# Two graph attention layers on one core: a transpose put ahead of the scores, the norm done in pairs, x split in five pieces, and a limit on list parts

## The chip, the core and the metric

The kernel runs on one core of a Trainium2 chip. A core has TensorE (PE in the profile; PEld is its loading of weights), VectorE (DVE), ScalarE (ACT), GpSimd (POOL) and SyncE (SP), which here issues the transfers. The engines run side by side, each through its own list of instructions in order, and wait for one another through semaphores. The metric is the device time of one execution in microseconds (us); lower is better.

## The reference

Sixteen graphs (batches) of 1024 nodes, 64 features each, with an adjacency matrix `adj` in which a node has itself and a handful of neighbours. Two layers, each with a residual and a layer norm without weights:

```python
# layer 0: attention with 8 heads of 64, over the neighbours only
q, k, v = (x @ Wq + bq), (x @ Wk + bk), (x @ Wv + bv)        # per head
scores  = leaky_relu(q k^T / 8 + edge_bias[edges], 0.2)       # -1e9 where edges == 0
out     = softmax(scores) v
x       = layernorm(x + out @ Wp + bp)
# layer 1: additive attention, one head
hp = x @ lin_w^T + lin_b;  u = hp @ W1^T;  w = hp @ W2^T
e  = sum_f a_f * leaky_relu(u_i + w_j, 0.2)                   # -9e15 where adj == 0
x  = layernorm(x + elu(softmax(e) hp))
```

## The kernel before

The kernel never forms 1024 x 1024 scores. For every batch it reads the adjacency matrix once and makes a list of neighbours for each node. Then both layers gather the listed neighbours with matmuls against indicator matrices and work on 120 slots for each group of nodes.

**Lists.** `prepare(b)` makes the lists of batch b in 41 pieces: it reads `adj` (L324, L327), folds it with matmuls (`pat`, L333, L338), finds the largest keys by pairs of MAX8 and MATCH_REPLACE (L344/L345, later L377/L379), turns keys into columns (L352 to L367, tiles `left`, `flags`) and writes out columns and slots. `finish(b)` makes the `mask` (L427 to L442).

**Gathering.** A layer needs x in three bf16 parts, whose sum is x in full precision: `thirds` (L451 cast, L453 what is left, five GpSimd instructions). For every tile t of 128 nodes `indicate` makes the indicator tiles `f` on VectorE (L475, two of [128 x 2176]), `gather` runs the matmuls with the parts (L499) in two halves, `own` copies each node's own column (L484, GpSimd), and `turn` transposes what was gathered (L518).

**Layer 0, tile t.** `queries` (L586, L587), `score` (matmuls L603, then on VectorE `sc` L611, `ls` L619, `mx` L620), `exps` (ACT, L629), `divide` (reciprocal L636 on VectorE, product L637 on GpSimd, in two halves 0 and 1), `turn_weights` (L645, L647), `attend` (L655), for every second tile `heads` (`po`, L671), `rows` (L687), and `residual` (L693, then `look`: BN statistics L544, L545). `end()` runs `Norm.scale` on the whole batch: four GpSimd instructions L549 (add), L550 (pow), L551 (subtract), L552 (multiply), and gives `x1`.

**Layer 1, tile t.** `own_rows` (`ub`, L728, GpSimd), `project` (`pz` L740 and L746, then `r` on ACT L751 and VectorE L752), `weigh` (`e`, L766, then its maximum `m1`, L768), `exps` (L774), `turn_weights` (transpose `pt1` L780, copy `eT` on VectorE L782), `attend` (`pa`, L791), `rows` and `residual` (L804, L805). `end()` is a generator: ELU, residual (L819, L820), `look` for all tiles, `Norm.scale`, output.

**Order.** The order on every engine is written out by hand in one loop over g = 0 to 146, under a manual schedule. Batch and tile are `b, t = divmod(g, 8)`. Layer 0 works on tile g and finishes it up to three steps later; layer 1 runs LAG = 12 steps behind (u = g - 12). At five places in each step, `lists.place(g, k)` puts in pieces of the next lists, up to a due number (3 to 6 a step by `QUOTA`, two steps ahead), and one piece of the first generator in `lists.side` (`finish`, or layer 1's `end`). `Layer0(b + 1)` is created at the end of t = 6 and `Layer1(b - 1)` at the end of t = 2; the constructor calls `begin`, which transposes x (`px`, L274) and makes the three parts.

Three PSUM tiles share one single bank, tag "e" of the pool `ps_z`: `back` (the rows of both layers), `e` in `weigh`, and `pt1` in `turn_weights`. A tile gets it when the readers of the tile before are through. The middle of a step, as written before the change:

```python
lists.place(g, 1)
at(l1, u, "gather", 0)
at(l0, g - 1, "turn")
lists.place(g, 2)
at(l1, u - 1, "weigh")
...
at(l1, u, "gather", 1)
...
at(l0, g - 2, "turn_weights")
at(l1, u - 2, "turn_weights")
at(l1, u - 1, "turn")
```

Of the kernel before, what the change touches and what calls it, by code (L numbers as in the profile page):

```python
# [24 lines left out]
WIN = 34  # L25
# [8 lines left out]
def kernel(  # L34
# [244 lines left out]
            for n in range(2):  # L279
                nc.tensor.matmul(ps[sub(n), t, :], src[:, ts(t, D)], w(n), start=True, stop=True)  # L280

    started, edges, masks, late = {}, {}, {}, {}

    def start(b):

        xs = dbl.tile([P, NT, D], F32, tag="xs", bufs=3, name=f"xs_{b}")
        dg = sml.tile([P, NT], I32, tag="dg", bufs=2, name=f"dg_{b}")
        diag = adj[b].rearrange("r c -> (r c)")[0 : N * N : N + 1]
        for n in range(2):
            nc.sync.dma_start(xs[sub(n), :, :], by_rows(x[b], n))  # L290
# [15 lines left out]
        started[b] = xs, dg, ads, load  # L306

    def prepare(b):

        if b not in started:  # L310
            start(b)
        xs, dg, ads, load = started.pop(b)
# [99 lines left out]
        for n in range(2):  # L412
            for q in range(NQ):
# [6 lines left out]
        edges[b] = (xs, col_d)  # L420
        late[b] = (flags, dg, rows_s)

    def finish(b):

        flags, dg, rows_s = late.pop(b)
        mask = dbl.tile([P, NT, SLOTS], BF16, tag="mask", bufs=4, name=f"mask_{b}")
# [8 lines left out]
        nc.vector.tensor_scalar(mask[:, :, 2 * CAP2 : SLOTS], own, 0.0, NEG, ALU.is_equal, ALU.mult)  # L435
        yield
        nc.vector.tensor_scalar(dgf, dg, 2.0, None, ALU.is_ge)
        nc.vector.tensor_reduce(flags[:, 18:19], dgf, XX, ALU.max)
        fl = sml.tile([P, 1], F32, tag="fl", bufs=2, name=f"fl_{b}")
        nc.vector.tensor_reduce(fl, flags, XX, ALU.max)  # L440
        nc.vector.tensor_scalar(fl, fl, 0.5, None, ALU.is_ge)
        nc.vector.tensor_tensor(bad, bad, fl, ALU.max)  # L442
        masks[b] = mask

    def thirds(src, tag, nm):

        t3 = dbl.tile([P, 3, NT, D], BF16, tag=tag, bufs=3, name=f"{tag}_{nm}")
        rest = src
        less = per.tile([P, NT, D], F32, tag="less", name=f"less_{tag}_{nm}")
        for k in range(3):  # L450
            nc.gpsimd.tensor_copy(t3[:, k, :, :], rest)  # L451
            if k < 2:
                nc.gpsimd.tensor_tensor(less, rest, t3[:, k, :, :], ALU.subtract)  # L453
                rest = less
        return t3

    class Tiles:


        def load(self, t):  # L460
            nm = f"{self.b}_{self.layer}_{t}"
            self.cb[t] = cb = dbl.tile([P, NSEG, 2, NQ, WIN], BF16, tag="cb", bufs=3, name=f"cb_{nm}")
            nc.sync.dma_start(
                cb.rearrange("p s n q k -> p (s n q k)"),
                self.col_d[t].rearrange("s n q k -> (s n q k)").unsqueeze(0).to_broadcast([P, NSEG * 2 * NQ * WIN]),
            )

        def indicate(self, t):
# [52 lines left out]
        def begin(self, x_):  # L521

            b = self.b
            px = ps_g.tile([P, 512], F32, tag="g", name=f"px{self.layer}_{b}")
            columns_T(px, x_)
            self.xT = dbl.tile([P, 512], F32, tag=f"xT{self.layer}", name=f"xT{self.layer}_{b}")
            nc.scalar.copy(self.xT, px)
            self.t3 = thirds(x_, "x3", f"{self.layer}_{b}")
            self.f, self.xg, self.xn = {}, {}, {}

    def banks(tag, name):

# [2 lines left out]
    class Norm:  # L535
# [8 lines left out]
            nc.vector.bn_stats(s6, y[:, t, :])  # L544
            nc.vector.bn_aggr(self.mv[:, t, :], s6)  # L545

        def scale(self, dst, y):
            rs = sml.tile([P, NT], F32, tag="rs", name=f"rs_{self.nm}")
            nc.gpsimd.tensor_tensor(rs, self.mv[:, :, 1], eps.to_broadcast([P, NT]), ALU.add)  # L549
            nc.gpsimd.tensor_tensor(rs, rs, root.to_broadcast([P, NT]), ALU.pow)  # L550
            nc.gpsimd.tensor_tensor(dst, y, self.mv[:, :, 0:1].to_broadcast([P, NT, D]), ALU.subtract)  # L551
            nc.gpsimd.tensor_tensor(dst, dst, rs.unsqueeze(2).to_broadcast([P, NT, D]), ALU.mult)  # L552

    class Layer0(Tiles):
        layer = 0

        def __init__(self, b):
            self.b, self.cb, (self.xs, self.col_d) = b, {}, edges[b]
            self.begin(self.xs)
            self.mx = dbl.tile([P, 2, NG // 4], F32, tag="mx", name=f"mx_{b}")  # L560
            self.y = dbl.tile([P, NT, D], F32, tag="y", name=f"y0_{b}")
            self.norm = Norm(f"0_{b}")
            self.qp, self.ls, self.den, self.w = {}, {}, {}, {}

# [125 lines left out]
        def residual(self, t):  # L690
            if t % 2 == 0:
                return
            nc.vector.tensor_tensor(self.y[:, t - 1 : t + 1, :], self.pr, self.xs[:, t - 1 : t + 1, :], ALU.add)  # L693
            for t_ in (t - 1, t):
                self.norm.look(self.y, t_)

        def end(self):
            x1 = dbl.tile([P, NT, D], F32, tag="x1", name=f"x1_{self.b}")
            self.norm.scale(x1, self.y)

            low = sml.tile([P, 1], F32, tag="low", bufs=2, name=f"low_{self.b}")
            nc.vector.tensor_reduce(low, self.mx.rearrange("p n g -> p (n g)"), XX, ALU.max)
            nc.vector.tensor_scalar(low, low, -NEG / 100.0, None, ALU.is_gt)
            nc.vector.tensor_tensor(bad, bad, low, ALU.max)
            return x1

    class Layer1(Tiles):
        layer = 1

        def __init__(self, b, x1):  # L710
            self.b, self.cb, self.x1, (_, self.col_d) = b, {}, x1, edges[b]
# [5 lines left out]
        def sums(self):  # L717
            pu = ps_g.tile([P, NT, D], F32, tag="g", name=f"pu_{self.b}")
            for t in range(NT):
                for n in range(2):  # L720
                    nc.tensor.matmul(pu[sub(n), t, :], self.xT[:, ts(t, D)], w1h[:, n, :], start=True, stop=True)
            self.u = dbl.tile([P, NT, D], F32, tag="u", name=f"u_{self.b}")
# [86 lines left out]
        def end(self):  # L809
# [10 lines left out]
            nc.gpsimd.tensor_tensor(y, y, self.x1, ALU.add)  # L820
            yield
            norm = Norm(f"1_{b}")
            for t in range(0, NT, 2):
                norm.look(y, t)
                norm.look(y, t + 1)
                yield
            norm.scale(o, y)
            yield
            for n in range(2):
                nc.sync.dma_start(by_rows(out[b], n), o[sub(n), :, :])  # L830

# [14 lines left out]
    class Lists:  # L846
# [11 lines left out]
        def place(self, g, k):  # L858
            b, t = divmod(g + AHEAD, NT)
            due = PIECES * b + sum(QUOTA[:t]) + QUOTA[t] * (k + 1) // PLACES  # L860
            last = k == PLACES - 1
            while self.done < due and self.part != ("keys" if last else "sums"):
                self.part = next(self.work, None)
                self.done += 1
            while self.side:
# [6 lines left out]
    with tc.manual_schedule(engines={getattr(mybir.EngineType, e) for e in order}):  # L872
        for _ in prepare(0):
            pass
        for _ in finish(0):
            pass
        l0[0] = Layer0(0)
        l0[0].constants()
        l0[0].load(0)
        l0[0].load(1)  # L880
# [2 lines left out]
        for g in range(NT * B + LAG + 7):  # L883
            u = g - LAG
            b, t = divmod(g, NT)
            if t == 0 and 0 < b < B:
                lists.side.append(finish(b))
            lists.place(g, 0)
            at(l0, g - 2, "exps", 0, range(4))
            at(l0, g - 1, "score", lambda: at(l0, g - 2, "divide", 0))  # L890
            if (g - 1) // NT not in l0:
                at(l0, g - 2, "divide", 0)
            at(l0, g - 2, "exps", 1, range(2))
# [4 lines left out]
            back = ps_z.tile([P, 3, D], F32, tag="e", name=f"back_{g}") if g > 3 else None  # L898
            at(l1, u - 3, "rows", back)
            at(l0, g - 3, "rows", back)  # L900
            at(l0, g, "queries")
            at(l1, u - 3, "residual")
            at(l0, g - 3, "residual")
            if t == 6 and b - 2 in l1:
                lists.side.append(l1[b - 2].end())
            at(l0, g - 2, "divide", 1)
            at(l1, u - 1, "project")
            lists.place(g, 1)
            at(l1, u, "gather", 0)
# [7 lines left out]
            if t == 2 and b - 1 in l0:  # L917
                x1 = l0[b - 1].end()
            at(l0, g - 2, "turn_weights")
            at(l1, u - 2, "turn_weights")  # L920
            at(l1, u - 1, "turn")
            lists.place(g, 3)
            at(l1, u + 1, "indicate")
# [433 lines left out]
```

## Time and profile before

| | |
|---|---|
| median of 3 runs | 2505.18 us (2500.58 to 2507.12) |
| the profiled execution | 2508.74 us, its span 2506.8 us |
| granted TensorE clock in it | 0.988 of full speed |
| busy time of PE, DVE, ACT, POOL | 92%, 80%, 58%, 36% of the span |
| costliest VectorE line | f, L475: 512 instructions, 491.6 us |
| costliest GpSimd line | ls, L637: 256 instructions, 285.8 us |
| longest waits of PE in the loop | po for sc 27.7 us, e for r 17.7 us, pz for sc 17.1 us |

The profile is one execution. A line of a timeline gives the start, the duration, the engine, the line of the kernel, the operation, `out<-in` by tile names with shapes, and in brackets the idle time before it with what ended it. A line of windows gives for one stretch its length and the busy time of each engine with the number of instructions, then the granted clock and the share of the DMA engines. A table of waits names who waited for whom, the total, the count and the longest.

### The profile page before, as it was taken

Reading aid. Unit: us, or ns where it says so; the run is one execution under the profiler, and the core shown is the slowest. Engines: PE = TensorE matmul, PEld = TensorE weight load, DVE = VectorE, ACT = ScalarE, POOL = GpSimd, SP = SyncE. Lnnn points to the kernel's source line nnn. Section 1 sums busy time; section 2 is a strip of 40 time slices with the busy share of each in tenths; the row PEclk is TensorE's granted clock in tenths of the full one; section 3 lists DMA queues with packets and bytes.
Section 4 is the critical chain, followed back from the end, with each engine's and each line's share of the span. In section 5 each row is a group of like instructions: output and inputs, shape, how many; then the busy total and the mean of one; then the engine's idle time right before and its main releaser. Section 6 shows DMA issues by size and latency. Waiting matters only on the chain. (4 is left out here: it accounts for less than half of the span.)

```text
span 2506.8 us, 110853 instructions
## 1 busy us (share of the span) xinstructions
PE 2308.1 (92%) x48706; PEld 1957.7 (78%) x48706; DVE 2012.1 (80%) x5237; ACT 1445.2 (58%) x4401; POOL 912.9 (36%) x1106
## 2 busy tenths in 40 slices
PE   5387999999999999999999999999999999999986
PEld 3376788878788887878788787888878888888864
DVE  6687879888888988888898888889888888876642
ACT  0154656656565665656566566656656665666743
POOL 1133333434334343433434343342434434243331
PEclk9998999999999999999999999999999999999998
DMA  3412332423233242323324232332423233221210
GB/s 102 122 59 89 104 103 78 133 77 116 73 102 108 78 133 80 114 73 107 103 78 133 84 109 75 106 103 78 133 86 108 81 100 106 62 92 57 66 52 18
DMA packets 190543, 230.66 MB, mean 92 GB/s; under 512 B 91492, under 2 KB 157092, under 8 KB 190052
## 3 DMA queue, kind: packets, MB, share of 16 engines
q1 hardware_dynamic: 190052, 223.49, 28.3%
q8 instruction: 384, 6.29, 1.0%
q14 instruction: 107, 0.88, 0.1%
HBM read 218.23 MB, written 5.21 MB: 89 GB/s over the span
## 5 line engine op out<-in xcount | busy, mean ns | idle before, releaser
L499 PE MATMUL pg<-f,x 128*64 128x272 bf16 (+2 forms) x13312 | 804.5, 272 | 37.4 <-DVE f L475 34.5
L499 PEld LDWEIGHTS <-x 128*64 128x64 bf16 x13312 | 662.0, 109 | 115.5 <-issue 70.4
L637 POOL TENSOR_TENSOR ls<-ls,den 128x480 f32<-128x480 f32 x256 | 285.8, 1117 | 921.1 <-DVE den L636 912.6
L475 DVE TENSOR_SCALAR f<-cb,jrow 128x2176 bf16<-128x2176 bf16 x512 | 491.6, 1001 | 0.3 <-DMA cb<-col_d 0.3
L505 ACT COPY xg<-pg 128x448 f32<-128x448 f32 x512 | 271.5, 530 | 356.1 <-PE pg L499 355.1
L629 ACT ACTIVATE ls<-ls,mx 128x120 f32<-128x120 f32 x1024 | 391.2, 386 | 4.8 <-DVE mx L620 4.8
L519 ACT COPY xn<-pt 120x512 f32<-120x512 f32 x512 | 277.3, 597 | 11.8 <-PE pt L518 7.1
L751 ACT ACTIVATE r<-pz 128x480 f32<-128x480 f32 x256 | 132.1, 568 | 247.0 <-PE pz L746 247.0
L518 PE MATMUL pt<-ident,xg 128*120 128x128 f32 x2048 | 273.9, 276 | 0.0
L484 POOL COPY xg<-xT 128x64 f32<-128x64 f32 x256 | 107.2, 426 | 387.9 <-PE pt L518 345.4
L518 PEld LDWEIGHTS pt<-ident,xg 128*120 128x120 f32 x2048 | 224.0, 137 | 27.3 <-issue 24.8
L752 DVE SCALAR_TENSOR_TENSOR r<-pz,r 128x480 f32<-128x480 f32 x256 | 155.4, 649 | 50.6 <-ACT r L751 50.6
L629 ACT ACTIVATION_READ_ACCUMULATOR ls<-ls,mx 128x1 f32 x1024 | 194.8, 190 | 0.0
L619 DVE SCALAR_TENSOR_TENSOR ls<-sc 128x480 f32<-128x480 f32 x256 | 191.5, 748 | 0.0
L620 DVE TENSOR_REDUCE mx<-ls 128x4 f32<-128x480 f32 x256 | 167.2, 653 | 8.8
L611 DVE TENSOR_TENSOR sc<-s,rowc 128x480 f32<-128x480 f32 x256 | 155.1, 647 | 22.7 <-PE s L603 21.0
L746 PEld LDWEIGHTS pz<-rw,ub 64*64 64x64 f32 x4096 | 122.6, 133 | 63.9 <-issue 58.5
L655 PE MATMUL z<-w,xn 120*64 120x64 f32 x4096 | 159.2, 227 | 4.4 <-ACT w L647 4.4
L587 DVE TENSOR_TENSOR qp<-pq,qb 128x512 f32<-128x512 f32 x128 | 87.9, 686 | 90.0 <-PE pq L586 89.8
L655 PEld LDWEIGHTS z<-w,xn 120*64 120x64 f32 x4096 | 138.4, 139 | 27.7 <-ACT w L647 19.4
L645 PE MATMUL pp<-ident,ls 128*120 128x128 f32 x1024 | 142.0, 280 | 19.3 <-POOL ls L637 16.6
L740 PE MATMUL pz<-xg,w2d 64*64 64x480 f32 x1024 | 140.4, 588 | 17.1 <-DVE sc L611 17.1
(212 smaller groups left out, 3881.1 us busy)
## 6 DMA issues: line engine op xcount, KB each, us to landing
cb<-col_d SPq DMA_DIRECT2D x256, 544.0 KB
ad<-in_adj_dram SPq DMA_DIRECT2D x256, 256.0 KB
xs<-in_x_dram SPq DMA_DIRECT2D x32, 128.0 KB
rows_s<-slot_d SPq DMA_DIRECT2D x256, 14.0 KB
out_dram<-o SPq DMA_DIRECT2D x32, 128.0 KB
col_d<-col SPq DMA_DIRECT2D x128, 4.2 KB
dg<-in_adj_dram SPq DMA_DIRECT2D x32, 2.0 KB
slot_d<-slot SPq DMA_DIRECT2D x16, 28.0 KB
```

What stands on the lines that cost most here:

```text
L475: nc.vector.tensor_scalar(fj.rearrange("p s n q k -> p (s n q k)"), cb.rearrange("p s n q k -> p (s n q k)"), jrow[:, j : j + 1], None, AL ...
L499: nc.tensor.matmul(pg[sub(n), :, FIRST * a_ + lo : FIRST * a_ + to], self.t3[:, k, 4 * hs + 2 * a_ + j, :], f[j][:, 2 * hs + a_, n, :, lo:to],
L505: nc.scalar.copy(dst, pg)
L518: nc.tensor.transpose(pt[:, q, :], xg[:, 4 * m + q, :], ident)
L519: nc.scalar.copy(self.xn[t][:, ts(m, 4), :], pt)
L611: nc.vector.tensor_tensor(sc, both[n], self.rowc[:, n, ts_].unsqueeze(2).to_broadcast([P, 4, SLOTS]), ALU.add)
L619: nc.vector.scalar_tensor_tensor(ls, scs[n], SLOPE, scs[n], ALU.mult, ALU.max)
L620: nc.vector.tensor_reduce(self.mx[:, n, ts_], ls, XX, ALU.max, negate=True)
L629: nc.scalar.activation(ls[:, q, :], ls[:, q, :], AF.Exp, bias=neg[:, q : q + 1], accum_out=den[:, q : q + 1])
L637: nc.gpsimd.tensor_tensor(ls, ls, den.unsqueeze(2).to_broadcast([P, 4, SLOTS]), ALU.mult)
L655: nc.tensor.matmul(zz[sub(n), q, :], xn[:, q, sub(n)], w_[n][:, q // 2, sub(q % 2)], start=True, stop=True)
L752: nc.vector.scalar_tensor_tensor(r, pz[n], SLOPE / (1.0 - SLOPE), r, ALU.mult, ALU.add)
```

## The change

Four things are changed.

1. Layer 1's `turn_weights(u - 2)` moves from behind layer 0's `turn_weights` to right behind the first half of layer 1's gather, ahead of `turn` of layer 0 and `weigh` of layer 1. The tile `back` is taken from its pool earlier in the step.
2. `Norm.scale` works on pairs of tiles: two looks, then the four GpSimd instructions on two tiles. Layer 0's are called in `residual` of every odd tile and write y in place (`x1` is gone, `y` has three buffers); layer 1's `end()` has two yields for each pair.
3. `thirds` returns its five instructions as a generator that goes to the front of `lists.side`, so that one is put in at each place. `Layer0(b + 1)` is created at the end of t = 4 instead of t = 6; its first load stays at t = 6.
4. A place puts in at most two list parts, except the last place of the step whose due tile is 7.

To find room, `mask` goes from four buffers to three, and layer 1's `xT` and `u` from two to one. `finish(b)` goes to the front of `lists.side`.

```diff
@@ thirds
         less = per.tile([P, NT, D], F32, tag="less", name=f"less_{tag}_{nm}")
-        for k in range(3):
-            nc.gpsimd.tensor_copy(t3[:, k, :, :], rest)
-            if k < 2:
-                nc.gpsimd.tensor_tensor(less, rest, t3[:, k, :, :], ALU.subtract)
-                rest = less
-        return t3
+
+        def parts(rest):
+            for k in range(3):
+                nc.gpsimd.tensor_copy(t3[:, k, :, :], rest)
+                yield
+                if k < 2:
+                    nc.gpsimd.tensor_tensor(less, rest, t3[:, k, :, :], ALU.subtract)
+                    rest = less
+                    yield
+
+        return t3, parts(src)
@@ begin
-            self.t3 = thirds(x_, "x3", f"{self.layer}_{b}")
+            self.t3, parts = thirds(x_, "x3", f"{self.layer}_{b}")
             self.f, self.xg, self.xn = {}, {}, {}
+            lists.side.insert(0, parts)
@@ Norm
-        def scale(self, dst, y):
-            rs = sml.tile([P, NT], F32, tag="rs", name=f"rs_{self.nm}")
-            nc.gpsimd.tensor_tensor(rs, self.mv[:, :, 1], eps.to_broadcast([P, NT]), ALU.add)
-            nc.gpsimd.tensor_tensor(rs, rs, root.to_broadcast([P, NT]), ALU.pow)
-            nc.gpsimd.tensor_tensor(dst, y, self.mv[:, :, 0:1].to_broadcast([P, NT, D]), ALU.subtract)
-            nc.gpsimd.tensor_tensor(dst, dst, rs.unsqueeze(2).to_broadcast([P, NT, D]), ALU.mult)
+        def scale(self, dst, y, t):
+            two = slice(t - 1, t + 1)
+            for t_ in (t - 1, t):
+                self.look(y, t_)
+            rs = sml.tile([P, 2], F32, tag="rs", name=f"rs_{self.nm}_{t}")
+            nc.gpsimd.tensor_tensor(rs, self.mv[:, two, 1], eps.to_broadcast([P, 2]), ALU.add)
+            nc.gpsimd.tensor_tensor(rs, rs, root.to_broadcast([P, 2]), ALU.pow)
+            nc.gpsimd.tensor_tensor(
+                dst[:, two, :], y[:, two, :], self.mv[:, two, 0:1].to_broadcast([P, 2, D]), ALU.subtract
+            )
+            nc.gpsimd.tensor_tensor(
+                dst[:, two, :], dst[:, two, :], rs.unsqueeze(2).to_broadcast([P, 2, D]), ALU.mult
+            )
@@ Layer0.residual
-            for t_ in (t - 1, t):
-                self.norm.look(self.y, t_)
+            self.norm.scale(self.y, self.y, t)
@@ Layer0.end
-            x1 = dbl.tile([P, NT, D], F32, tag="x1", name=f"x1_{self.b}")
-            self.norm.scale(x1, self.y)
...
-            return x1
+            return self.y
@@ Layer1.end
-            for t in range(0, NT, 2):
-                norm.look(y, t)
-                norm.look(y, t + 1)
+            for t in range(1, NT, 2):
+                norm.scale(o, y, t)
                 yield
-            norm.scale(o, y)
-            yield
+                yield
@@ Lists.place
-            while self.done < due and self.part != ("keys" if last else "sums"):
+            end = self.done + 2 if (t, k) != (NT - 1, PLACES - 1) else due
+            while self.done < min(due, end) and self.part != ("keys" if last else "sums"):
@@ the loop over g
             at(l1, u, "gather", 0)
+            at(l1, u - 2, "turn_weights")
             at(l0, g - 1, "turn")
...
             at(l0, g - 2, "turn_weights")
-            at(l1, u - 2, "turn_weights")
             at(l1, u - 1, "turn")
...
+            if t == 4 and b + 1 < B:
+                l0[b + 1] = Layer0(b + 1)
             if t == NT - AHEAD and b + 1 < B:
-                l0[b + 1] = Layer0(b + 1)
                 l0[b + 1].load(0)
```

More of the change, by code (lines that the diff above doesn't have):

```diff
@@ L280, in rows_T @@
                 nc.tensor.matmul(ps[sub(n), t, :], src[:, ts(t, D)], w(n), start=True, stop=True)
-    started, edges, masks, late = {}, {}, {}, {}
+    inputs, started, edges, masks, late = {}, {}, {}, {}, {}
     def start(b):
@@ L305, in start @@
             load(k)
-        started[b] = xs, dg, ads, load
+        inputs[b] = xs
+        started[b] = dg, ads, load
     def prepare(b):
@@ L311, in prepare @@
             start(b)
-        xs, dg, ads, load = started.pop(b)
+        dg, ads, load = started.pop(b)
         flags = sml.tile([P, 32], F32, tag="flags", bufs=2, name=f"flags_{b}")
@@ L419, in prepare @@
                 )
-        edges[b] = (xs, col_d)
+        edges[b] = col_d
         late[b] = (flags, dg, rows_s)
@@ L425, in finish @@
         flags, dg, rows_s = late.pop(b)
-        mask = dbl.tile([P, NT, SLOTS], BF16, tag="mask", bufs=4, name=f"mask_{b}")
+        mask = dbl.tile([P, NT, SLOTS], BF16, tag="mask", bufs=3, name=f"mask_{b}")
         nc.vector.tensor_scalar(mask[:, :, 0 : 2 * CAP2], rows_s, code, NEG, ALU.not_equal, ALU.mult)
@@ L447, in thirds @@
         t3 = dbl.tile([P, 3, NT, D], BF16, tag=tag, bufs=3, name=f"{tag}_{nm}")
-        rest = src
         less = per.tile([P, NT, D], F32, tag="less", name=f"less_{tag}_{nm}")
-        for k in range(3):
-            nc.gpsimd.tensor_copy(t3[:, k, :, :], rest)
-            if k < 2:
-                nc.gpsimd.tensor_tensor(less, rest, t3[:, k, :, :], ALU.subtract)
-                rest = less
-        return t3
+        def parts(rest):
[7 more added lines that the diff above has]
+        return t3, parts(src)
     class Tiles:
@@ L464, in load @@
                 cb.rearrange("p s n q k -> p (s n q k)"),
-                self.col_d[t].rearrange("s n q k -> (s n q k)").unsqueeze(0).to_broadcast([P, NSEG * 2 * NQ * WIN]),
+                edges[self.b][t].rearrange("s n q k -> (s n q k)").unsqueeze(0).to_broadcast([P, NSEG * 2 * NQ * WIN]),
             )
@@ L525, in begin @@
             columns_T(px, x_)
-            self.xT = dbl.tile([P, 512], F32, tag=f"xT{self.layer}", name=f"xT{self.layer}_{b}")
+            self.xT = dbl.tile([P, 512], F32, tag=f"xT{self.layer}", bufs=2 - self.layer, name=f"xT{self.layer}_{b}")
             nc.scalar.copy(self.xT, px)
-            self.t3 = thirds(x_, "x3", f"{self.layer}_{b}")
+            self.t3, parts = thirds(x_, "x3", f"{self.layer}_{b}")
             self.f, self.xg, self.xn = {}, {}, {}
+            lists.side.insert(0, parts)
     def banks(tag, name):
@@ L557, in __init__ @@
         def __init__(self, b):
-            self.b, self.cb, (self.xs, self.col_d) = b, {}, edges[b]
+            self.b, self.cb, self.xs = b, {}, inputs[b]
             self.begin(self.xs)
             self.mx = dbl.tile([P, 2, NG // 4], F32, tag="mx", name=f"mx_{b}")
-            self.y = dbl.tile([P, NT, D], F32, tag="y", name=f"y0_{b}")
+            self.y = dbl.tile([P, NT, D], F32, tag="y", bufs=3, name=f"y0_{b}")
             self.norm = Norm(f"0_{b}")
@@ L710, in __init__ @@
         def __init__(self, b, x1):
-            self.b, self.cb, self.x1, (_, self.col_d) = b, {}, x1, edges[b]
+            self.b, self.cb, self.x1 = b, {}, x1
             self.begin(x1)
@@ L721, in sums @@
                     nc.tensor.matmul(pu[sub(n), t, :], self.xT[:, ts(t, D)], w1h[:, n, :], start=True, stop=True)
-            self.u = dbl.tile([P, NT, D], F32, tag="u", name=f"u_{self.b}")
+            self.u = dbl.tile([P, NT, D], F32, tag="u", bufs=1, name=f"u_{self.b}")
             nc.vector.tensor_tensor(self.u, pu, rows_b[:, 0:1, :].to_broadcast([P, NT, D]), ALU.add)
@@ L877 @@
         l0[0] = Layer0(0)
+        for _ in lists.side.pop():
+            pass
         l0[0].constants()
@@ L886 @@
             if t == 0 and 0 < b < B:
-                lists.side.append(finish(b))
+                lists.side.insert(0, finish(b))
             lists.place(g, 0)
@@ L892 @@
                 at(l0, g - 2, "divide", 0)
+            back = ps_z.tile([P, 3, D], F32, tag="e", name=f"back_{g}") if g > 3 else None
             at(l0, g - 2, "exps", 1, range(2))
@@ L897 @@
             at(l0, g - 2, "exps", 1, range(2, 4))
-            back = ps_z.tile([P, 3, D], F32, tag="e", name=f"back_{g}") if g > 3 else None
             at(l1, u - 3, "rows", back)
@@ L901 @@
             at(l0, g, "queries")
+            if t == 6 and b - 2 in l1:
+                lists.side.append(l1[b - 2].end())
             at(l1, u - 3, "residual")
             at(l0, g - 3, "residual")
-            if t == 6 and b - 2 in l1:
-                lists.side.append(l1[b - 2].end())
             at(l0, g - 2, "divide", 1)
```

## Prediction

> **What bounds the kernel now.** I read the page's first part, then cut the span into steps from one layer-0 score to the next, then looked at each long step in the timeline, and last at the table of waits.
>
> ```profile
> PE 2308.1 (92%) x48706; PEld 1957.7 (78%) x48706; DVE 2012.1 (80%) x5237; ACT 1445.2 (58%) x4401; POOL 912.9 (36%) x1106
> ```
>
> TensorE is busy for 92% of the span. The windows of one batch, t = 1 to 7 and then t = 0 of the loop, with a window of the last batch's tail behind them, show where it is not:
>
> ```profile
> core 0: us, PE busy (x) PEld busy (x) DVE busy (x) ACT busy (x) POOL busy (x), PEclk, DMA share, GB/s
> 1366.90:1384.30 17.40, 17.40 (x347) 14.41 (x346) 12.24 (x26) 12.56 (x43) 6.31 (x9) 1.00 0.56 183
> 1384.30:1404.80 20.50, 18.81 (x414) 16.06 (x413) 18.01 (x51) 9.79 (x28) 10.42 (x12) 1.00 0.09 32
> 1404.80:1423.90 19.10, 17.45 (x374) 15.05 (x373) 18.64 (x45) 12.00 (x39) 6.00 (x8) 1.00 0.24 70
> 1423.90:1442.30 18.40, 17.67 (x381) 14.86 (x379) 15.88 (x43) 10.57 (x31) 3.77 (x5) 1.00 0.41 126
> 1442.30:1457.90 15.60, 15.60 (x344) 13.73 (x341) 13.31 (x32) 10.87 (x33) 3.84 (x5) 1.00 0.13 39
> 1457.90:1475.80 17.90, 17.90 (x415) 15.60 (x413) 14.51 (x36) 12.02 (x37) 5.32 (x6) 1.00 0.29 74
> 1475.80:1494.50 18.70, 18.48 (x411) 15.37 (x409) 17.08 (x44) 12.59 (x43) 16.34 (x20) 1.00 0.60 201
> 1494.50:1512.10 17.60, 17.45 (x378) 14.87 (x377) 15.14 (x42) 9.58 (x27) 4.58 (x5) 1.00 0.21 66
> 2321.60:2338.50 16.90, 16.90 (x380) 14.69 (x377) 12.19 (x27) 11.80 (x36) 4.00 (x5) 1.00 0.20 68
> ```
>
> The batch takes 145.2, about thirteen such follow one another. A step that is all TensorE is 15.6 (t=5), with heads 16.9 (last line). Adding the batch's extra matmuls to these (px 1.0, sums 1.0, transposed adjacency 1.9, constants 1.1, estimates from the matmul counts) gives 137.8. So 7.4 us a batch are lost: 2.6 at t=2, 2.5 at t=3, 1.5 at t=4, 0.7 at t=0. At t=3 VectorE is busy for 18.64 of 19.10; there it, not TensorE, sets the step.
>
> At t=2 a burst of list parts stands in front of the score's eviction:
>
> ```profile
> 1384.43 0.69 DVE L338 SCALAR_TENSOR_TENSOR ka<-pat,revc 128x512 f32<-128x512 f32 x1 [2.99 <-PE pat L333]
> ...
> 1386.03 0.42 DVE L344 MAX8 lst<-ka 128x8 f32<-128x256 f32 x1
> ...
> 1386.88 0.16 DVE L352 TENSOR_SCALAR flags<-lst 128x4 f32<-128x4 f32 x1
> ...
> 1387.41 1.22 DVE L611 TENSOR_TENSOR sc<-s,rowc 128x480 f32<-128x480 f32 x2
> 1388.12 0.43 PE L671 MATMUL po<-zT,wvp 64*64 64x128 f32 x2 [1.02 <-DVE sc L611]
> ```
>
> sc starts 3.1 after the score, and TensorE waits 1.02 for its bank. From 1402.3 the five GpSimd parts of layer 1's x run beside VectorE:
>
> ```profile
> 1403.02 1.20 POOL L453 TENSOR_TENSOR less_x<-x,x 128x512 f32<-128x512 f32 x1
> 1403.23 1.02 DVE L364 TENSOR_SCALAR left<-left 128x32 int32<-128x32 int32 x1
> ```
>
> The same L364 takes 0.18 at 1396.58: it ends when GpSimd's instruction ends. The pair of f (L475), 1.47 undisturbed at 1418.64, takes 2.24, 2.73 and 3.10 beside GpSimd. So sc of t=3 starts only 5.9 after its score.
>
> **Transposes in front of the scores.** pt1 (L780) and its copy eT (L782, 0.28) move ahead of weigh. What leaves: attend's wait for eT (0.54 at t=2; 5.9 in the whole trace) and pt1's wait for ACT's exponentials (6.4). What comes: e (L766) takes over the one bank of tag "e" and must wait for the eT copy, which stands on VectorE behind r (L752) and the pieces of place 1. At t=0:
>
> ```profile
> 1503.58 1.22 DVE L752 SCALAR_TENSOR_TENSOR r<-pz,r 128x480 f32<-128x480 f32 x2 [0.24 <-ACT r L751]
> ...
> 1505.39 0.62 PE L766 MATMUL e<-r,a_two 128*32 128x120 f32 x16
> ...
> 1506.08 0.20 DVE L435 TENSOR_SCALAR mask<-own 128x64 bf16<-128x64 f32 x1
> 1506.19 0.42 DVE L344 MAX8 lst<-ka 128x8 f32<-128x256 f32 x1
> ...
> 1509.51 0.28 DVE L782 COPY eT<-pt 120x128 f32<-120x128 f32 x1
> ```
>
> e starts 0.59 after r ends (1504.80); that is all the cover there is. Place 1 puts 1.39 there (1504.80 to 1506.19), the copy 0.28: e starts at about 1506.5, +1.1, less the 0.11 of pt1 that now lies ahead of it: **+1.0 at t=0**. One list pair of MAX8 and MATCH_REPLACE (0.91) gives 0.91 + 0.28 - 0.59 - 0.11 = **+0.5 at t=4**. At t=7 the two L324 (0.75) and one pair of looks (0.72) stand there; r itself comes about 1.2 earlier, since one of two pairs of looks leaves the front of sc (0.67) and L619 (1.61 at 1481.01, against 0.76) loses most of its lock. e then starts about 10.5 after the score instead of 9.8: **+0.6**. t=1 has a short piece: **+0.2**. At t=5 the piece is covered. Queued behind the waiting e on TensorE are gather 1, the weights' turn and attend, so the wait counts in full where the step is TensorE's.
>
> **Norm by pairs.** Out of t=2 go 0.20 + 1.68 + 1.10 + 1.04 = 4.0 of GpSimd, out of t=7 4.8. For them come eight times four instructions. A pair's tile has 128 elements a partition; the trace has 0.24 for a copy of 64 (L484), 0.42 to 0.55 for 128 in bf16 (L327), 1.04 to 1.10 for 512: I take 0.36 to 0.4 for subtraction and for product (0.24 to 1.1). pow on two elements has only the row of eight (L550, 1.68) above and L549 (0.20, an add) below: I take 0.55, the share of a work that grows with the elements; the ends stay for the range. A pair is then 1.6, hidden on GpSimd between divide 0 (ends 1390.1 at t=2) and divide 1 (1394.92), whose result TensorE needs only after gather 1; divide 1 goes 1.6 later without being late. If that cover were gone, the pp transposes wait.
>
> Does pow block VectorE? In the trace it does not: from 1396.14 to 1397.8 L362 to L365 ran at 0.17 to 0.19. The Trainium skill, page "SBUF — State Buffer", section "Who interferes with whom", has one exclusive shared pair of ports, held for the whole instruction. By it pow would block L363 and L365 (two inputs in SBUF) like the others, and eight pairs a batch would cost up to about 2 us a batch more; this row disagrees, and I go by the row.
>
> **Parts of x in five.** 4.6 us of GpSimd (0.6, 1.2, 0.6, 1.2, 1.0) leave the end of t=2 and t=6 and spread over the five places of t=3 and t=5. px's matmuls (1.0) go from t=6 to t=4: zero in sum. Each part blocks what VectorE has beside it, f above all: at t=5 I put **+0.4**, felt at t=6, where sc starts 1.9 instead of 1.4 after the score. In t=3 the parts' locks leave VectorE late at t=4: **+0.6** (0 to 1.0; below nothing if VectorE's freed time covers it all).
>
> **Two list parts at most.** In a steady batch one place changes: t=2 place 0. The second pair of L344/L345 (0.85) and L352 to L358 (0.53) go to place 1, between r and eT. sc and po come sooner by up to 1.4, e waits for eT at 12.2 to 12.8 after the score, as late as r's chain has it now, and pa's 0.54 falls away: **-0.8 at t=2**.
>
> At t=3 the norm's and parts' locks that now delay VectorE (0.77 on f, 0.56 on L704, 0.84 on L364, 0.46 on L365, 0.43 more on the next f) go: 2.5 to 3. sc starts 3.4 after the score instead of 5.9, r follows 4.88 later as now, e waits about 1.0 for eT behind its 0.91 pair instead of 2.5 in all: **-1.5 at t=3**.
>
> **The sum.** A batch: -0.8 - 1.5 + 0.5 + 0.6 + 0.4 + 0.6 + 1.0 + 0.2 = +1.0; thirteen: +13. Ten steps at the end with layer 1 alone (9.13 each, e waits 0.41 for r now) get 0.25 each: +2.5. The last norm's shorter chain after eight more looks: +0.5. At the start layer 0's first parts, and layer 1's first norms, stand earlier: -2 (0 to -5). +14.0 on the profiled execution's 2508.74 (span 2506.8 and 1.94 around it) is 2522.7. That execution is 3.56 over the median of the runs, so I forecast 2519.2 for the median.
>
> **Rivals.**
> First, faster: VectorE's lag of t=2 to t=4 vanishes. Its work there without locks is 47.3 of TensorE's 51.4. If the locks do not come back in t=3, only the eT waits are left: t=2 -1.6, t=3 -2.0, t=4 -0.9, then +0.4, +0.6, +1.0 and +0.2 as above: -2.3 a batch, -30 and 1 elsewhere: 2476. It decides where sc starts under 2.7 after the score at t=3 and under 1.5 at t=4. For it speaks that 6.6 of the 7.4 lost lie there; against it that eT's waits are new in nearly every step.
> Second, slower still: pow of two elements costs like that of eight (1.7), so a pair is 2.7. It then lies over place 1 and the f behind it; L367 under such a lock took 0.93 instead of 0.19 (1398.01). Two such in front of eT a batch are +1.5: 14 + 19.5 gives 2539.
> Third, gains and losses meet: without the two lags (0.6 at t=4, 0.4 at t=6) the batch's sum is zero, and 1 us is left elsewhere: about 2506. For it speaks that the parts of x are spread and VectorE is busy for only 13.3 of 15.6 at t=5; against it that a lock stretches f wherever it meets one.
>
> **How the numbers follow.** The forecast of about 2519 with its neighbours has 0.35, pow at full price 0.15, the meeting 0.17, the first rival 0.33. Low 2470 takes in the first rival and the start's -5; high 2545 the second with part of the lag. About 0.3% (7.5 us) is what a measurement of this kernel tells from no change. Faster 0.33, same 0.17, slower 0.50. Outcomes of both signs hold most of the chance; the likeliest one's own range is 2513 to 2530.
>
> **What would show it.** Right: in the waits, PE e waits on DVE eT, in tens of microseconds, and po's wait on sc falls; t=3 shrinks to about 17.6, t=0 grows to 18.6, t=4 to 20.5 (1.0 of it px); L550 on two elements at 0.5 to 0.6. Wrong: e waits on r as before and not on eT; t=4 at 19.4 or less with px in it; pow at 1.7, or VectorE blocked during it; a new wait of pp on GpSimd's ls.

## The result, and the profile after

The changed kernel takes 2508.99 us (median of 20 runs, 2502.66 to 2513.54) against 2504.21 before (20 runs, 2499.86 to 2508.27): a ratio of 1.002, 95% interval 1.0012 to 1.0028. It is slower by about 5 us, within the 0.3% (7.5 us) that the prediction took for no change; +14 was forecast. The sign was right and the size was not; that the sign was right is luck, as the parts below show. The profiled execution took 2508.34 us, its span 2506.5.

The first part of its page:

```profile
PE 2296.7 (92%) x48706; PEld 1951.9 (78%) x48706; DVE 1930.4 (77%) x5237; ACT 1450.3 (58%) x4401; POOL 1010.8 (40%) x1490
```

VectorE's time falls by 82 us, though it does the same 5237 instructions: f (L475, now L480) alone goes from 491.6 to 409.0 us. GpSimd's rises by 98. The windows of one batch, t = 1 to 4, then t = 6, 7 and 0:

```profile
core 0: us, PE busy (x) PEld busy (x) DVE busy (x) ACT busy (x) POOL busy (x), PEclk, DMA share, GB/s
1226.20:1243.80 17.60, 17.45 (x350) 14.36 (x349) 12.45 (x25) 12.61 (x43) 6.58 (x10) 1.00 0.64 195
1243.80:1263.40 19.60, 18.29 (x414) 15.86 (x413) 17.13 (x54) 9.74 (x27) 5.94 (x10) 1.00 0.11 35
1263.40:1280.80 17.40, 16.55 (x370) 14.61 (x369) 16.92 (x47) 11.96 (x38) 8.56 (x9) 1.00 0.27 75
1280.80:1299.50 18.70, 18.32 (x416) 15.84 (x412) 16.12 (x43) 10.86 (x33) 6.30 (x10) 1.00 0.49 146
...
1315.00:1332.00 17.00, 17.00 (x383) 14.74 (x381) 14.05 (x33) 11.81 (x36) 8.09 (x12) 1.00 0.39 93
1332.00:1351.30 19.30, 18.49 (x412) 15.38 (x409) 14.04 (x40) 12.54 (x43) 13.40 (x22) 1.00 0.68 209
1351.30:1370.10 18.80, 17.44 (x378) 14.86 (x377) 16.26 (x47) 9.60 (x27) 7.72 (x13) 1.00 0.14 51
```

This batch takes 143.9 where 145.2 stood before; each is among the shortest of its execution, and the means of twelve batches are 145.1 and 145.8. t=2, t=3 and t=6 are shorter, t=0 and t=7 longer, and t=4 has px's 1.0 in it and is hardly longer. The waits of TensorE over the whole span:

```profile
PE e L776 <- DVE eT L792: 73.2, 90, 1.9
...
PE po L684 <- DVE sc L624: 4.6, 3, 2.9
```

The wait that the forecast named is there, the largest of the loop, and po's wait for sc falls from 27.7 to 4.6. At t=0 the timeline shows what stands in front of the copy:

```profile
1360.39 1.22 DVE L762 SCALAR_TENSOR_TENSOR r<-pz,r 128x480 f32<-128x480 f32 x2 [0.24 <-ACT r L761]
...
1363.23 0.20 DVE L436 TENSOR_SCALAR mask<-own 128x64 bf16<-128x64 f32 x1
1363.34 0.28 DVE L792 COPY eT<-pt 120x128 f32<-120x128 f32 x1
1363.68 0.62 PE L776 MATMUL e<-r,a_two 128*32 128x120 f32 x16 [1.30 <-DVE eT L792]
```

So the steady batches became shorter, and yet the run became longer: the loss is ahead of them. From here on scores are counted from 0, and step n goes from score n to score n + 1, so that step 16 is a t=1. In the two traces the score of step 16 starts at 344.7 before and at 356.1 after, +11.4. From there to step 112 the change gains 9.1, and behind that 2.6, so the two profiled executions end within 0.3 of each other. That of before was 4.5 slower than its median and that of after 0.7 faster than its own, which is the rest of the 5 us.

### The profile page after: what moved, and what is told of

Its sections match the earlier page's. It is cut to its first block, busy times and chain, and to the rows that moved or that the text cites. A ratio compares the mean times of both kernels' runs of the same rounds, so it can differ in the third digit from the quotient of the medians.

```text
span 2506.5 us, 111153 instructions
## 1 busy us (share of the span) xinstructions
PE 2296.7 (92%) x48706; PEld 1951.9 (78%) x48706; DVE 1930.4 (77%) x5237; ACT 1450.3 (58%) x4401; POOL 1010.8 (40%) x1490
## 4 chain that ended last, share of the span: by engine, by line
PE 66%; DVE 25%; DMA 3%; ACT 2%; issue 2%; POOL 1%; SPq 0%; POOLq 0%; ACTq 0%; DVEq 0%
PE pg L504 21%; PE s L616 5%; PE pt L523 5%; PE z L668 5%; DVE r L762 4%; PE pz L750 4%; PE pp L658 4%; PE pa L801 4%; PE pq L599 4%; PE pz L756 4%; PE po L684 3%; PE e L776 3%; DVE f L480 3%; DMA ad<-in_adj_dram 2%; PE pat L334 2%
## 5 line engine op out<-in xcount | busy, mean ns | idle before, releaser
L650 POOL TENSOR_TENSOR ls<-ls,den 128x480 f32<-128x480 f32 x256 | 298.5, 1166 | 579.8 <-DVE den L649 577.0
L480 DVE TENSOR_SCALAR f<-cb,jrow 128x2176 bf16<-128x2176 bf16 x512 | 409.0, 843 | 1.2 <-DMA cb<-col_d 1.0
L523 PEld LDWEIGHTS pt<-ident,xg 128*120 128x120 f32 x2048 | 229.4, 138 | 7.3 <-ACT xg L510 2.8
L489 POOL COPY xg<-xT 128x64 f32<-128x64 f32 x256 | 98.8, 396 | 307.1 <-PE pt L523 307.1
L558 POOL TENSOR_TENSOR rs<-mv,eps 128x2 f32<-128x2 f32 x128 | 32.3, 253 | 379.0 <-DVE den L649 299.4
L632 DVE SCALAR_TENSOR_TENSOR ls<-sc 128x480 f32<-128x480 f32 x256 | 175.7, 686 | 0.0
```

What stands on the lines that cost most here:

```text
L480: nc.vector.tensor_scalar(fj.rearrange("p s n q k -> p (s n q k)"), cb.rearrange("p s n q k -> p (s n q k)"), jrow[:, j : j + 1], None, AL ...
L523: nc.tensor.transpose(pt[:, q, :], xg[:, 4 * m + q, :], ident)
L632: nc.vector.scalar_tensor_tensor(ls, scs[n], SLOPE, scs[n], ALU.mult, ALU.max)
L650: nc.gpsimd.tensor_tensor(ls, ls, den.unsqueeze(2).to_broadcast([P, 4, SLOTS]), ALU.mult)
```

## The experiments

Ratios are to the kernel before, with 95% intervals. Step lengths are medians over the twelve batches between the scores of steps 16 and 112, in us, by t of the loop; "16" is the start of that step's score in the profiled execution. The runs that are not in the table are in the text.

| kernel | 16 | t=1 | 2 | 3 | 4 | 5 | 6 | 7 | 0 | median us |
|---|---|---|---|---|---|---|---|---|---|---|
| before | 344.7 | 17.66 | 20.40 | 19.09 | 18.44 | 15.56 | 17.93 | 18.77 | 17.57 | 2504.21 |
| after | 356.1 | 17.83 | 19.59 | 17.48 | 18.65 | 15.56 | 16.95 | 19.35 | 18.77 | 2508.99 |
| e1 | 346.8 | 17.71 | 20.91 | 17.00 | 18.64 | 15.56 | 16.95 | 19.34 | 18.76 | 2510.05 |
| e2 | 353.4 | 17.86 | 19.51 | 16.86 | 19.77 | 15.56 | 17.24 | 18.47 | 18.56 | 2494.72 |
| e4 | 356.3 | 17.42 | 19.53 | 16.60 | 19.78 | 15.56 | 16.95 | 18.46 | 18.58 | 2491.25 |
| e7 | 345.1 | 17.78 | 19.25 | 17.48 | 18.65 | 15.56 | 16.95 | 19.35 | 18.46 | 2495.19 |
| e8 | 344.5 | 17.70 | 20.11 | 20.50 | 17.59 | 15.56 | 17.93 | 19.35 | 17.93 | 2524.72 |
| e10 | 342.4 | 17.40 | 20.43 | 16.54 | 19.78 | 15.56 | 17.24 | 18.74 | 17.57 | 2485.03 |
| e12 | 345.8 | 17.40 | 19.76 | 19.33 | 18.45 | 15.56 | 17.93 | 18.84 | 16.95 | 2496.63 |
| e9 | 340.9 | 18.69 | 18.18 | 17.68 | 19.78 | 15.56 | 16.95 | 18.51 | 16.95 | 2468.03 |
| e13 | 337.2 | 17.42 | 17.93 | 17.34 | 18.87 | 15.56 | 16.95 | 18.59 | 16.95 | 2430.38 |

**e1: no limit of two.**

```diff
-            end = self.done + 2 if (t, k) != (NT - 1, PLACES - 1) else due
-            while self.done < min(due, end) and ...
+            while self.done < due and ...
```

> The kernel after without the limit of two list parts at a place. Theory (the loss is the start, +10 us before step 16, and the waits of e for eT, about 2.3 us a batch, against gains of 2.4 us at t=2 and t=3): the first step's list parts come at once again, so the score of step 8 comes some 4 us sooner than 220; at t=2 sc is later again but two pieces leave the front of eT, so that step changes by 0 to +0.8 us. Together -4 to +6 us against the kernel after: 2505 to 2515 us. Rival (the limit itself is what costs): the start's 10 us go and the time falls to 2499 us or less.

2510.05 us, 1.0023 (1.0013 to 1.0033): as the kernel after. But two effects cancel. Step 16 comes 9.3 sooner, and t=2 and t=3 together are 0.8 longer in each batch: sc of t=2 starts 3.1 after its score, as in the kernel before, instead of 1.7. The prediction had no term for what the limit does at the start.

**e2: transposes back behind layer 0's.**

```diff
-            at(l1, u - 2, "turn_weights")
             at(l0, g - 1, "turn")
...
             at(l0, g - 2, "turn_weights")
+            at(l1, u - 2, "turn_weights")
```

> The kernel after with layer 1's turn_weights where it was before (behind layer 0's). Theory: e waits for r alone again; t=0 loses 1.1 us, t=7 0.6, t=1 0.2, t=4 0.4, t=3 up to 0.5: about 2.5 us a batch, and 2 us in the steps of layer 1 alone: about 2474 us. Rival (pt1 behind e has waits of its own, for ACT's exponentials and attend for eT, that give it back): no more than 10 us: 2499 us or more.

2494.72 us, 0.996 (0.9946 to 0.9975): 14 us better than after, less than half of what was expected, and 4 us past the rival's bound. t=7 and t=3 fall by 0.9 and 0.6, but t=4 rises by 1.1, and t=0 falls by 0.2 only: there pt1 waits for ACT's exponentials (26.2 us in all), as the rival had it.

**e4: place 1 behind the transposes**, so that the copy stands right behind r.

```diff
-            lists.place(g, 1)
             at(l1, u, "gather", 0)
             at(l1, u - 2, "turn_weights")
+            lists.place(g, 1)
```

> The kernel after with the list parts of place 1 put behind layer 1's turn_weights, so that the copy eT stands on VectorE right behind r. Theory: e no longer waits for eT, the gains at t=2 and t=3 stay: t=0 -1.1 us, t=7 -0.6, t=1 -0.2, t=4 -0.4, some at t=2 and t=3: 2.5 us a batch or a little more, about 2474 us. Rival (the wait is the bank's, whose transpose and copy lie on the way in any case): 2500 us or more, and PE e still waits tens of us on DVE eT.

2491.25 us, 0.9945 (0.9928 to 0.9963). This is 18 us less than after, where 35 were expected. e's wait for eT falls from 73.2 to 6.8 us, but at t=0 another wait, of 1.02 instead of 1.30, takes its place. From the table of waits of this kernel, and then from its timeline at t=0:

```profile
PE pt L523 <- ACT xg L510: 22.2, 26, 1.0
```

```profile
1501.63 0.19 DVE L550 BATCH_NORM_STATS2 st<-y 128x6 f32<-128x64 f32 x1
...
1501.96 0.25 DVE L778 TENSOR_REDUCE m<-e 128x1 f32<-128x120 f32 x1
...
1503.17 0.65 PE L523 MATMUL pt<-ident,xg 128*120 128x128 f32 x4 [1.02 <-ACT xg L510]
```

The maximum m now stands behind a list pair, flags and two looks of layer 1's norm. ACT waits for m before its exponentials, and its copy xg is queued behind them, so TensorE waits 1.02. And t=4 takes 19.78, as in e2.

**e3 and e15: the second load.** Something that neither the diff's words nor the prediction had: with `Layer0(b + 1)` made at t=4, the loop's own `at(l0, g + 2, "load")` already loads its tile 0 at t=6, and the old line at the step's end loads it again: 271 transfers of `cb` instead of 256.

```diff
# e3, on the kernel after
-            if t == NT - AHEAD and b + 1 < B:
-                l0[b + 1].load(0)
# e15, on the kernel before
                 l0[b + 1].load(0)
+                l0[b + 1].load(0)
```

> The kernel after without the second of two loads of tile 0's columns: since Layer0(b + 1) now exists at t=6, the loop loads its tile 0 in the middle of t=6 and then again at the end of that step, 15 extra transfers of 544 KB. Theory: they are hidden; 0 to -1 us, 2508 to 2509 us. Rival (they delay the adjacency's transfers, so that t=7 and t=1 of some batches come out 0.6 to 1.6 us longer): those steps all take 19.35 and 17.62 us, -5 us, 2504 us.

> The kernel before with a second load of each batch's tile 0 columns, 15 transfers of 544 KB more. Theory (the 4 us between the kernel after and e3_one_load are these transfers'): 3 to 5 us slower than before. Rival (that difference was the scatter of the runs): within 1.5 us of before.

e3: 2504.84 us, 0.9998 (0.9989 to 1.0008), 4 less than after. e15: 2507.56, 1.001 (1.0001 to 1.0019), 2.5 more than before. Both speak for a cost of 2 to 4 us, at the edge of what can be told. The traces do not show where: the medians of the steps are alike, and e3's profiled execution was itself no faster. From step 16 to step 112 e3's execution takes 3.4 less than after's and e15's 1.7 more than before's, which fits, but one execution of each does not prove it. The rival's place, t=7 and t=1, is not confirmed. These two runs also show how far one reading of the start can be trusted: up to step 16 each differs from its base by two transfers, and yet e3's score of step 16 comes 3.5 later and e15's 5.1 sooner.

**e7: the pair's norm behind the second divide.**

```diff
             at(l0, g - 2, "divide", 1)
+            at(l0, g - 3, "normalise")        # the four GpSimd instructions, out of residual
```

> The kernel after with layer 0's four GpSimd instructions for a pair behind the second divide instead of in front of it. Theory (at the start layer 1 has no work yet, so that the transposes pp reach the second half of the weights before the delayed divide has made it: pp waits 3.2 us instead of 1.0): the score of step 8 comes 6 us sooner than at 220; in the steady batch divide was hidden, 0. About 2503 us. Rival (the start's loss is the limit's alone): the score of step 8 at 218 or later, 2508 us or more.

2495.19 us, 0.9967 (0.9957 to 0.9978): 14 us less than after by the medians. In the two traces 11.0 of it are up to step 16 (8.9 up to step 8, where 6 were expected), and 0.3 a batch each at t=2 and t=0. What the edit takes away stands in the timeline of an early step, in the kernel after:

```profile
157.39 0.19 POOL L558 TENSOR_TENSOR rs<-mv,eps 128x2 f32<-128x2 f32 x1 [4.32 <-DVE den L649]
157.66 0.71 POOL L559 TENSOR_TENSOR rs<-rs,root 128x2 f32<-128x2 f32 x1
158.34 0.40 POOL L560 TENSOR_TENSOR y<-y,mv 128x128 f32<-128x128 f32 x1
158.81 0.40 POOL L563 TENSOR_TENSOR y<-y,rs 128x128 f32<-128x128 f32 x1
159.17 1.53 POOL L650 TENSOR_TENSOR ls<-ls,den 128x480 f32<-128x480 f32 x1
...
160.75 1.11 PE L658 MATMUL pp<-ident,ls 128*120 128x128 f32 x4 [3.22 <-POOL ls L650]
```

and in the same step of e7:

```profile
155.82 0.99 POOL L648 TENSOR_TENSOR ls<-ls,den 128x480 f32<-128x480 f32 x1 [4.45 <-DVE den L647]
...
156.86 0.65 PE L656 MATMUL pp<-ident,ls 128*120 128x128 f32 x4 [1.02 <-POOL ls L648]
```

Layer 1 has nothing to do yet in these steps, so its projection and gather, which hide the divide later, are not there. The divide comes 1.8 later and is itself longer beside VectorE, and pp waits 2.2 more. This recurs at every second step: at steps 3, 5 and 7 the longest wait of pp is 1.0, 1.4 and 1.0 before, 3.2, 3.8 and 2.7 after, and 1.0, 1.4 and 1.0 in e7.

These waits are not the whole of the 11.4. Already the first score starts 3.9 later after than before; it starts at 105.0 to 107.0 in the six kernels with the limit at the start and at 101.9 to 103.2 in the others. And between the first score and step 8 the granted clock is lower, 0.87 against 0.92 (0.90 in e7), so that TensorE is busy 4.8 longer with the same work. The windows of that stretch, before and then after:

```profile
102.30:205.80 103.50, 83.76 (x1632) 71.45 (x1632) 85.63 (x227) 52.43 (x171) 28.96 (x36) 0.92 0.33 102
106.20:220.40 114.20, 88.53 (x1634) 74.52 (x1633) 89.56 (x232) 52.41 (x171) 33.01 (x49) 0.87 0.34 98
```

TensorE's idle time grows by 5.9 there. Up to step 16 the parts are +3.9 for the first score, +5.2 of busy time at the lower clock and +2.3 of idle time. Why the clock is lower there, no run shows; from step 16 to step 112 it is 1.00 in every run.

**e8, e10, e12: one part alone on the kernel before** (the move of the transposes; the five parts with one load; the norm by pairs as in the change). e10 also keeps the change's smaller edits: the buffer counts, `back` taken earlier and `finish` in front. Of these only the earlier `back` is in e8 too, and none was run by itself.

> The kernel before with only the move of layer 1's turn_weights (and the bank of back taken earlier). Theory: what stands at place 1 between r and eT is added to every step of TensorE's: t=0 +1.1, t=7 +1.1 (four looks there), t=4 and t=1 0.2 to 0.5, t=3 and t=2 about 0, since VectorE sets them: +2.5 us a batch, 2530 to 2540 us. Rival (what is late at eT was late anyway): +1 us a batch or less, 2518 us or less.

> The kernel before with only the parts of x in five pieces and Layer0(b + 1) at t=4 (one load of its tile 0). Theory (t=2 to t=4 together are VectorE's, whose locks go, so that px of 1.0 fits there for nothing, and t=6 gives 1.0 back): t=2 to t=4 from 57.9 to 57 at most, t=6 -1.0, t=7 -0.3: -1.5 to -2 us a batch, 2480 to 2486 us. Rival (the locks only move into t=3 and t=5, and px is paid in t=4): within 5 us of 2505.

> The kernel before with only the norm by pairs, in front of the second divide as in the change. Theory: the start loses 9 to 11 us up to step 16 (pp waits for the divide), and t=2, t=3 and t=7 of a batch, from which 4.0 and 4.8 us of GpSimd go, win 1 us together: 2495 to 2505 us. Rival (pairs cost more than the whole in every step, since pow is paid eight times): +5 us or more beyond the start's loss, 2518 us or more.

The transposes alone cost 19 us (1.0083, 1.0063 to 1.0103), between the two expectations: t=7 and t=0 lose 0.9 together, t=3 1.4, and t=4 gives 0.8 back; e waits 55.5 us for eT. The parts alone gain 21 us (0.9916, 0.9893 to 0.994), as expected, with t=3 2.5 shorter and t=4 1.3 longer (1.0 is px). The pairs alone gain 9 us (0.9964, 0.9951 to 0.9977): t=2 and t=0 win 0.6 each, and the start loses 1.1 to step 16, not the 9 to 11 expected, although the score of step 8 is 9.7 late there (215.5 against 205.8). What pairs lose early, this kernel wins back by step 16, at step 8 above all: pp waits there 4.0 and 2.2 before, 0.3 and 0.5 in e12, but 0.3 and 2.2 after. Added, the three give -11, and the second load about +3; the whole is +5, so some 13 us lie in how they meet. It is not the limit: e1, which has all but that, is also at +5. Nor is it the start: from step 16 to step 112 the three traces add up to -15.9 and e1's gives -1.2. What e1 and after have in common is t=0, where the medians of the three add up to -0.3 and both have +1.2. That what pairs alone gain there (16.95, all TensorE) is not to be had while e waits for eT is argued and not shown.

**e5, e6, e9, e11: put together.** e5 is e4 with one load and the limit only from g = 8. e6 adds place 2 behind `weigh` and its exponentials. e9 adds e7's edit. e11 is e9 with `QUOTA = (4, 3, 5, 6, 6, 5, 5, 7)`.

```diff
# e5
-            end = self.done + 2 if (t, k) != (NT - 1, PLACES - 1) else due
+            end = self.done + 2 if g >= NT and (t, k) != (NT - 1, PLACES - 1) else due
# e6
-            lists.place(g, 2)
             at(l1, u - 1, "weigh")
             at(l1, u - 1, "exps")
+            lists.place(g, 2)
```

> The kernel after with place 1 behind layer 1's turn_weights, one load of tile 0's columns, and the limit of two list parts only from g = 8 on. Theory (three separate losses: the limit costs 9 us at the start and saves 0.7 us a batch later, the second load 4 us, eT 18 us): the score of step 16 comes at about 347 us instead of 356; 2491 - 9 - 4 = about 2478 us. Rival (VectorE's work sets t=2 to t=4 and the lists' work left out of the start comes back there or in the next batch): no less than 2487 us.

> As e5_free_start, and the list parts of place 2 stand behind weigh and its exponentials. Theory: at t=0 layer 1's maximum m no longer stands behind a list pair, flags and two looks; ACT's exponentials and its copy of the gathered columns come sooner and the turn's wait of 1.0 us goes: t=0 falls from 18.6 to about 17.6, t=7 from 18.5 to 18.4 at most, about -1 us a batch, -13 us: about 2465 us where e5 gives 2478. Rival (the pieces then delay f, and the next gather or sc): t=0 stays at 18.6 or the next step gives it back; no difference to e5.

> As e6_maximum_first, and layer 0's norm of a pair behind the second divide (as in e7). Theory (the start's loss is the divide's, and does not depend on what else is changed): the score of step 16 comes 8 to 10 us sooner than at 348.8, and t=2 up to 0.3 a batch: 2472 less 10 to 14, about 2460 us. Rival (without the limit at the start the lists set the pace there): 2469 us or more.

> As e9_all_five, with one list part less due in each of t=3 and t=4 and one more in each of t=5 and t=6 (QUOTA 4, 3, 5, 6, 6, 5, 5, 7). Theory (VectorE's work sets t=2 to t=4, a pair of MAX8 and MATCH_REPLACE is 0.9 us of it, and t=5 and t=6 have VectorE idle for 2 us and more): t=3 and t=4 together 1 to 1.8 us shorter, t=5 and t=6 unchanged: 13 to 23 us less than e9. Rival (what holds t=3 and t=4 is one wait, po for sc, and not the amount of work): the same as e9 within 4 us.

e5: 2482.39 (0.9918, 0.9901 to 0.9934), between theory and rival, step 16 at 349.7. e6: 2472.25 (0.9882, 0.9861 to 0.9903), 10 less than e5 where 13 were expected: t=0 falls to 16.95, all TensorE, and t=2 to 18.19, while t=1 rises by 1.3, as the rival had it. e9: 2468.03 (0.9861, 0.9837 to 0.9886), between theory and rival: step 16 at 340.9, 7.9 sooner, but the median gains only 4. e11 missed, theory and rival both: 2508.65 (1.0016, 1.0003 to 1.0029), 40 worse than e9. Moving the due numbers moved parts in every step: t=1 +1.1, t=0 +0.6, t=7 +0.8, step 16 +11.4. Yet t=4 fell by 0.9 and t=3 rose by 0.9, by one pair of MAX8 and MATCH_REPLACE less or more in front of sc. So what the rival named, the place of sc in the queue, was tried next.

**e13, e14: place 0 behind the score and its evictions**, on e9 and on the kernel after.

```diff
-            lists.place(g, 0)
...
             at(l0, g - 1, "score", lambda: at(l0, g - 2, "divide", 0))
...
+            lists.place(g, 0)
```

> As e9_all_five, with the list parts of place 0 behind the score and its evictions instead of in front of them. Theory (what holds t=4 is the po wait for sc, 1.22 us, and sc stands behind list pairs on VectorE; after mx VectorE waits 1.3 us for pq in even steps, so that a pair costs nothing there): sc of t=4 starts 0.9 sooner, t=4 falls by 0.9, t=3 by up to 0.4: 2468 less 10 to 16, about 2455 us. Rival (VectorE's sum of work from t=2 to t=4 sets their 55.6 us, wherever it stands): t=2 to t=4 stay at 55.6, 2465 us or more.

> The kernel after with only that: place 0 behind the score and its evictions. Theory: e waits for eT as before and hides what sc gains in odd steps; t=4 has 0.4 of TensorE idle to win and t=2 some 0.3: -0.5 us a batch, about 2502 us. Rival (VectorE's sum): the same as the kernel after within 3 us.

t=4 in e9's timeline:

```profile
1400.37 0.43 DVE L380 MATCH_REPLACE8 kb<-lst,ka 128x280 f32<-128x280 f32 x1
1400.72 1.21 DVE L622 TENSOR_TENSOR sc<-s,rowc 128x480 f32<-128x480 f32 x2
1401.42 1.66 PE L682 MATMUL po<-zT,wvp 64*64 64x128 f32 x32 [1.22 <-DVE sc L622]
```

and in e13's:

```profile
1235.82 0.68 DVE L736 TENSOR_TENSOR u<-pu,rows_b 128x512 f32<-128x512 f32 x1
1236.42 1.21 DVE L622 TENSOR_TENSOR sc<-s,rowc 128x480 f32<-128x480 f32 x2
1237.12 1.66 PE L682 MATMUL po<-zT,wvp 64*64 64x128 f32 x32 [0.31 <-DVE sc L622]
```

One pair fewer in front of sc, and po waits 0.91 less. e13 takes 2430.38 us, 0.9701 (0.9682 to 0.9719): 38 us under e9, more than twice what was expected, since t=1 falls by 1.3 as well and t=2 to t=4 by 1.5. Their sum is 54.1, under the 55.6 that the rival held fixed, while VectorE's busy time in the three steps hardly changes (50.4 in e9, 49.9 in e13): VectorE's total is not the bound there. e14: 2494.84 (0.9958, 0.9944 to 0.9972), 14 under after, where 7 were expected. e13 is the best version of the study, 75 us under the kernel before.

## Why the prediction was right or wrong, step by step

**The sum.** The forecast had +13 for the batches, -2 for the start and +3 for the end. The two traces give -9.1 for twelve batches, +11.4 for the start and -2.6 for the end. So the loss that was forecast for the batches is not there, and the loss that was measured stands where a gain was forecast. The errors have opposite signs, and only this brings the total near +5; the sign was luck. Where the batch is taken apart, the 137.8 comes out only with px and the transposed adjacency counted twice each, which the text does not say.

**Right.** The forecast's terms of t=2 (-0.8), t=3 (-1.5), t=0 (+1.0) and t=1 (+0.2) met -0.8, -1.6, +1.2 and +0.2; t=7 (+0.6) met +0.6. The new wait, its place on VectorE behind place 1, and the fall of po's wait were as described. e4 confirms the cause: with the copy right behind r the wait is nearly gone. e8 confirms that the move by itself costs.

**Wrong: t=4.** The forecast put +0.5 for eT, +0.6 for VectorE's lag and 1.0 for px: 20.5. Measured were 18.65, which meets the prediction's own sign of being wrong (19.4 or less). The step that failed is the term for VectorE's lag, set beside the wait for eT. sc there starts 1.7 after its score instead of 2.9 (medians of the twelve batches), so that the loss of 1.5 that the step had before paid for px. The lag was counted beside t=3's wait for eT, and they are one delay: while TensorE waits for eT, VectorE works on and is no longer late at t=4. Where that wait is absent (e2, e4, e9, e10), sc starts 3.3 after the score and t=4 takes 19.77 or 19.78. So what e2 and e4 gained at t=3 they lost at t=4, until e13 put the list parts behind sc.

**Wrong: t=6.** The parts' locks at t=5 were to cost 0.4. t=6 became 16.95, all TensorE, px's 1.0 shorter: nothing was lost. sc starts there 1.3 after its score; 1.9 was forecast.

**Wrong: the start.** -2 was forecast, +11.4 came. The step that failed is "divide 1 goes 1.6 later without being late": this was read from a steady batch, and the cover, layer 1's work, is not there in the first twelve steps. The prediction even named what would wait (pp) if it were gone, but priced it nowhere. e7 gives the 11.0 back by that edit alone, e1 9.3 by the limit alone. The score of step 16 comes at 339.6 to 344.7 in the kernels with neither (before, e8, e10, e15), at 345.1 to 346.8 with one (e1, e7, e12), and at 353.4 to 359.6 with both (after, e2, e3, e4, e14). So the loss needs both, beyond the scatter of about 5 that e3 and e15 show. The longer waits of pp at steps 3, 5 and 7 come with the pairs, with or without the limit (3.2, 4.9 and 2.7 in e12); that e12 makes them up at step 8 because the next batch's lists are early fits this, but was only argued.

**Wrong: the end.** +3 was forecast for the steps of layer 1 alone and the last norm; from step 112 on the two traces give -2.6, but e3, whose end differs from that of after by one transfer, gives 0.0 there. So a gain is not shown, only that the loss did not come. No run was made for it.

**The pow.** 0.55 was taken for two elements, with 1.68 as the upper end; it took 0.69 alone. The second rival is out, and subtraction and product took 0.40 each, as assumed. As to whether pow blocks VectorE: in the trace of before, L363 and L365 began 47 times while it ran, and took 0.19 in 45 of them; the other two began in its last 0.03 and took 1.09, beside the subtraction behind it. The rule of the Trainium skill ("SBUF — State Buffer", "Who interferes with whom") that one engine fully blocks the other does not hold for pow in that direction. In the other it shows: beside f, pow is stretched. In the kernel after it took 1.11 to 1.27 in all 29 cases in which the two meet, and 0.69 to 0.73 in the other 99. From the timelines of VectorE and GpSimd in an early step of the kernel after, where it took 1.27:

```profile
185.63 1.45 DVE L480 TENSOR_SCALAR f<-cb,jrow 128x2176 bf16<-128x2176 bf16 x2
```

```profile
186.51 1.27 POOL L559 TENSOR_TENSOR rs<-rs,root 128x2 f32<-128x2 f32 x1
```

**The rivals.** The first (2476) asked that sc start under 2.7 at t=3 and under 1.5 at t=4. At t=3 it is 3.3, and at t=4 it came near with 1.7, but t=0 and t=7 lost 1.8 a batch, as the forecast's 1.6 had it. e13 shows that much of the 6.6 us of t=2 to t=4 named there can be had by another order: they fall from 57.9 to 54.1, with px's 1.0 in them. The third (about 2506) was nearest in size. Its condition, no lags at t=4 and t=6, was met; but its 1 us elsewhere was not, and the total came near by a gain in the batches against a loss at the start.

**Open.** Where the second load's 2 to 4 us lie, how the pairs and the limit hold each other up between steps 8 and 16, and why the granted clock is lower in the first steps after the change.

## What to carry to other kernels

A cover that is read from a steady stage must be looked for again in the stages before it fills: the same four instructions in front of a divide cost 0.6 us in a steady batch and, with the limit in place, 11 us in the first two. On an in-order engine the question is not how much work it has in a step but what stands ahead of the one result that another engine waits for; putting 0.9 us list parts behind sc instead of in front of it took 38 us off the run. And two waits that follow one another on the same pair of engines can be one delay, as here at t=3 and t=4, and not two terms.

## What the runs showed of the hardware that was not expected

GpSimd's pow took 1.66 us on 8 elements a partition and 0.69 on 2; from these two rows 0.37 for the instruction and 0.16 an element are an estimate. It did not slow VectorE's small operations with two inputs in SBUF (0.19 in 45 of 47 cases), but was itself stretched beside f: to between 1.11 and 1.27 on 2 elements, and to 2.11 in most cases on 8.
